# Three small operations of a fused state-space and attention kernel leave VectorE

## The chip, the cores and the metric

The kernel runs on one core of a Trainium2 chip. That core has five engines with a queue of instructions each, which they work off in order: TensorE (PE; its weight loads are a row of their own, PEld), VectorE (DVE), ScalarE (ACT), GpSimd (POOL) and SyncE (SP), which here only issues DMAs. An instruction that needs another engine's result waits for a semaphore, and everything behind it on its own engine waits with it. The metric is the device time of one execution in microseconds, the median of several runs; lower is better.

## The reference

The input x has 32 sequences of 256 tokens and 256 features. Two blocks follow each other, and their result is added to x.

The first is a selective scan. For every sequence, x is projected to 512 inner features and a gate; the inner features get a conditioning vector, a causal convolution of four taps, a SiLU and a layernorm over the 512 features. From the normalised `xn` come 16 values each of B, C and dt per token. The recurrence is

```python
dt = jnp.tanh(dt @ W_dt.T + b_dt) * 0.01
A = -jnp.tanh(A_log)
Ad = 1.0 + dt * A
h = jnp.clip(h * ad[:, :, None] + bd[:, :, None] * xt[:, None, :], -10.0, 10.0)
yt = jnp.einsum('bd,bdh->bh', ct, h)
```

with 256 steps, one per token. Its output, with a skip term, is gated and projected back to 256 features.

The second block is two layers, each of local attention (8 heads of 64, windows of 128 tokens that also see the window before) and a gated feed-forward (682 hidden features, GELU). Queries and keys are normalised per head, `t / clip(norm(t), 1e-12)`, scaled and rotated before the scores.

## The kernel before

**Groups and stages.** The 32 sequences are worked in four groups of eight. The scan of a group holds its state as 128 rows (16 states times 8 sequences) by 512 features. `group_scan` cuts its 256 steps into eight chunks of 32. While attention and feed-forward of one group run, the scan of the next one runs beside them. So the first group's scan runs alone at the start, the last group's attention alone at the end, and between them both share the engines. A pair of sequences in attention goes with one chunk of the scan.

**What sets the order.** `at(slot, function, ...)` puts a function of the scan into a numbered slot, counted in steps; `stage(n, i, ...)` does the same for attention and feed-forward; the loop at the end interleaves the two lists. That gives the program order. The framework then moves instructions of an engine against each other where their dependences allow, except those marked `tc.keep_in_program_order`. Tiles come from rings of a few buffers, and all eight PSUM banks are one ring (`ps_w`): a matmul that takes a bank waits until whoever read that bank's last content is done.

**The scan's layernorm, per chunk and half `j`.** The convolved features are turned by TensorE into PSUM (`tp_x`, L548). `norm_stats` (L555 on) takes mean and variance on VectorE (L558, L560), adds the epsilon (L562), and GpSimd raises it to the power -0.5 (L565); the result is the first column of `stat`. `norm_shift` (L571) makes minus mean times that factor on VectorE, the second column. `norm_apply` (L579) uses both as scale and bias of one ScalarE pass, which writes `xn`. GpSimd then applies the layernorm's weights (`norm_affine`, L586 and L587), and the rows go to DRAM (`xnd`), from where every step's row is read again, spread over the states (`xrep`, L685).

**The decay factors, per chunk.** From small sums (`bcd`) ScalarE takes the tanh (`decay_th`, L643); `decays` multiplies by a rate per row and adds one (L648), takes the running product `pd` (L650), its reciprocal (L653) and from it the factor `beta` (L654), with which ScalarE scales every `xrep` (L706). A step of the scan is then one VectorE instruction, an addition with limits (L716), and TensorE reads the state out (`y`, L728). The limits `lim` are the clip divided by the product (L660, L661, on GpSimd).

**Queries and keys.** `rotated` (L998 on) is called for q and k of each window of 128 tokens. ScalarE squares the projection (L1002); VectorE makes the two rotated parts (L1005, L1010) and sums the squares per head into `ss` (L1015), 128 rows by 8 heads, limited from below at 1e-24 (L1019). GpSimd adds the parts (L1013), raises `ss` to -0.5 (`rn`, L1021) and multiplies (L1022). TensorE transposes the result (L1028).

**Others that the text speaks of.** L1386 is the gelu on ScalarE, L1393 the product with the other half on VectorE (it frees the bank `pa`), L1047 the addition to the residual, L1252 and L1260 the softmax's sums and their reciprocal `rinv`, L1271 the weighted values `ov`, L799 the scan's gate `zT`, L758 its skip product.

Of the kernel before, what the change touches and what calls it, by code (L numbers as in the profile page):

```python
# [10 lines left out]
FP = mybir.dt.float32  # L11
BF = mybir.dt.bfloat16
I32 = mybir.dt.int32
AF = mybir.ActivationFunctionType
ALU = mybir.AluOpType
# [4 lines left out]
P = 128  # L20
# [53 lines left out]
def kernel(  # L74
# [29 lines left out]
    nc = tc.nc  # L104
# [38 lines left out]
    a_sb = per_state(a_log, "a_sb")  # L143
# [24 lines left out]
    one = const.tile([P, 1], FP, tag="one", name="one")  # L168
# [53 lines left out]
    def program(ctx, exact):  # L222
# [3 lines left out]
        sm = ctx.enter_context(tc.tile_pool(name="sm", bufs=2, reuse_waits="tile"))  # L226
# [150 lines left out]
        def group_scan(g):  # L377
# [14 lines left out]
            def at(s, what, *args):  # L392
                agendas[-1].setdefault(s, []).append(partial(what, *args))
# [161 lines left out]
            def norm_stats(c, j):  # L555
                tp, stat = ck[c]["tp", j], ck[c]["stat"]
                st = sm.tile([P, 6], FP, tag="st", name="st")
                nc.vector.bn_stats(st, tp)  # L558
                mv = sm.tile([P, 2], FP, tag="mv", name="mv")
                nc.vector.bn_aggr(mv, st)  # L560
                ve = sm.tile([P, 1], FP, tag="ve", name="ve")
                nc.vector.tensor_scalar_add(  # L562
                    ve, mv[:, 1:2], LN_EPS if alone else 4 * LN_EPS
                )
                nc.gpsimd.tensor_tensor(stat[:, j, 0:1], ve, neg_half[:, 0:1], ALU.pow)  # L565
                ck[c]["mv", j] = mv

            def norm_shift(c, j):
                stat, mv = ck[c]["stat"], ck[c].pop(("mv", j))
                tc.keep_in_program_order(  # L570
                    nc.vector.scalar_tensor_tensor(  # L571
                        stat[:, j, 1:2], mv[:, 0:1], -1.0, stat[:, j, 0:1], ALU.mult, ALU.mult
                    )
                )

            def norm_apply(c, j):
# [64 lines left out]
            def decay_th(c):  # L641
                ad = sm.tile([P, CH], FP, tag="ad", name="ad")
                nc.scalar.activation(ad, ck[c]["bcd"][:, 2], AF.Tanh, bias=wbias[:, 2:3])  # L643
                ck[c]["ad"] = ad

            def decays(c):
                ad, bcd, beta = ck[c].pop("ad"), ck[c].pop("bcd"), ck[c]["beta"]
                nc.vector.tensor_scalar(ad, ad, a_sb, 1.0, ALU.mult, ALU.add)  # L648
                pd = sm.tile([P, CH], FP, tag="pd", name="pd")
                nc.vector.tensor_tensor_scan(pd, ad, zero_ch, state["p"], ALU.mult, ALU.add)  # L650
                state["p"] = pd[:, CH - 1 : CH]
                pi = sm.tile([P, CH], FP, tag="pi", name="pi")
                nc.vector.reciprocal(pi, pd)  # L653
                nc.vector.tensor_mul(beta, beta, pi)  # L654
                ct = sm.tile([P, CH], FP, tag="ct", name="ct")
                nc.vector.scalar_tensor_tensor(
                    ct, bcd[:, 1], wbias[:, 1:2], pd, ALU.add, ALU.mult
                )
                lim = sm.tile([P, 2, CH], FP, tag="lim", name="lim")
                nc.gpsimd.tensor_scalar_mul(lim[:, 0], pi, CLIP)  # L660
                nc.gpsimd.tensor_scalar_mul(lim[:, 1], pi, -CLIP)  # L661
                ck[c].update(ct=ct, lim=lim)
# [193 lines left out]
            for c in range(NCH):  # L856
                s0 = c * CH
                for hb in range(CH // TB):
                    s = s0 + hb * TB
                    for i in range(NI):  # L860
                        at(s + 4 * i + 5, read_out, c, hb, i)
                    at(s + 21, gated, c, hb)
                    at(s + 25, out_gate, c, hb)
                    at(s + 11, skip, c, hb)
                for ch in range(NC_):
                    at(s0 - 38 + 2 * ch, conv_in, c, ch)
                    at(s0 - 37 + 2 * ch, conv_taps, c, ch)
                    at(s0 - 36 + 2 * ch, conv_th, c, ch)
                    if not alone:
                        at(s0 - 35 + 2 * ch, conv_out, c, ch)  # L870
                for ch, s in enumerate((13, 16, 17, 18)):
                    at(s0 + s + 2, gate_th, c, ch)
                    if not alone:
                        at(s0 + s + 4, gate_out, c, ch)
                at(s0 - 25, raw_copy, c)
                at(s0 - 24, raw_turn, c)
                for j in range(NJ):
                    s = s0 - 26 + 4 * j
                    at(s + 2, norm_stats, c, j)
                    at(s + 4, norm_shift, c, j)  # L880
                    at(s + 5, norm_apply, c, j)
                    at(s + 6, norm_affine, c, j)
                    at(s + 9, norm_out, c, j)
                at(s0 - 11, length, c)
                at(s0 - 9, figures, c)
                at(s0 - 7, figures_in, c)
                at(s0 - 6, decay_th, c)
                at(s0 - 5, decays, c)
                at(s0 - 4, put_c, c, 0)
                at(s0 + 4, put_c, c, 1)  # L890
                for d in range(KM):
                    at(s0 + 45 + 2 * d, copy_y, c, d)
                    at(s0 + 46 + 2 * d, put_y, c, d)
# [104 lines left out]
        def rotated(l, ps, w, a):  # L998


            sq = ap_.tile([P, DI], FP, tag="swp", name="sq", bufs=3)
            nc.scalar.activation(sq, ps, AF.Square)  # L1002
            rot = ap_.tile([P, HEADS, DH], FP, tag="rot", name="rot", bufs=4)
            ph = ps.rearrange("p (h d) -> p h d", h=HEADS)
            nc.vector.tensor_mul(rot, ph, bc(rc_sb[:, l, w, a], 1, HEADS))  # L1005
            swp = ap_.tile([P, HEADS, DH], FP, tag="swp", name="swp", bufs=3)
            hd = DH // 2
            for i in range(2):
                o, s = slice(i * hd, (i + 1) * hd), slice((1 - i) * hd, (2 - i) * hd)
                nc.vector.tensor_mul(  # L1010
                    swp[:, :, o], ph[:, :, s], bc(rs_sb[:, l, w, a, o], 1, HEADS)
                )
            nc.gpsimd.tensor_add(rot, rot, swp)  # L1013
            ss = aw.tile([P, HEADS], FP, tag="ss", name="ss")
            nc.vector.tensor_reduce(  # L1015
                ss, sq.rearrange("p (h d) -> p h d", h=HEADS), AX.X, ALU.add
            )

            nc.vector.tensor_scalar_max(ss, ss, 1e-24)  # L1019
            rn = aw.tile([P, HEADS], FP, tag="rn", name="rn")  # L1020
            nc.gpsimd.tensor_tensor(rn, ss, neg_half, ALU.pow)  # L1021
            nc.gpsimd.tensor_mul(rot, rot, bc(rn, 2, DH))  # L1022
            return rot
# [638 lines left out]
```

## Time and profile before

| | us |
|---|---|
| median of 3 runs (lowest, highest) | 3594.73 (3590.82, 3597.36) |
| profiled execution, its own time | 3592.27 |
| its span | 3590.5 |
| TensorE busy | 3448.4 |
| VectorE busy | 2667.8 |
| ScalarE busy | 1979.5 |
| GpSimd busy | 1874.5 |

The span begins with the first instruction on the core and ends with the last. In the groups of instructions a row is one line of the kernel, its engine and operation, the tiles written and read, and the count; then the time busy in total, the mean of one in ns, the engine's idle time just before them and what ended most of it. Matmuls are pipelined, so the mean of one matmul is longer than its share. In a view of waits, "PE ov L1271 <- DVE ag L1393" is TensorE idle ahead of line 1271 until VectorE had finished line 1393, with the sum, the number of times and the longest. The chain that ended last follows the work back from the last instruction, at each step to what released it. TensorE's granted clock was 0.99 of full speed.

### The profile page before, as it was taken

The page shows a single profiled execution, that of the slowest core. Times are in us where ns is not written, and L with a number is a line of the kernel's source. Part 1 is how long each engine was busy: PE and PEld are TensorE (multiplying, and loading weights), DVE is VectorE, ACT ScalarE, POOL GpSimd, SP SyncE. Part 2 cuts the span into 40 slices and gives each one's busy share as a digit, 9 for nine tenths or more (in the row PEclk, how much of TensorE's full clock was granted, in tenths as well). Part 3 has the DMA queues.
Part 4 walks back from the last instruction along what each step waited for, and adds up shares of the span by engine and source line. Part 5 has one row for each costly group of instructions (what it writes and reads, how often), then busy time and mean ns, then how long its engine had stood idle before and what let it go on. Part 6 is the DMA issues. An engine that isn't in the chain of part 4 may idle for free.

```text
span 3590.5 us, 57544 instructions
## 1 busy us (share of the span) xinstructions
PE 3448.4 (96%) x20220; PEld 2253.8 (63%) x20220; DVE 2667.8 (74%) x5049; ACT 1979.5 (55%) x3535; POOL 1874.5 (52%) x1842
## 2 busy tenths in 40 slices
PE   7999989999999999999999999999999999999999
PEld 4545335566656666666666666666666677777777
DVE  5888989878788877877787888777777555555553
ACT  4656656656555655566566555665656444434442
POOL 4433467546556556655555566555545454544551
PEclk9999999999999999999999999999999999999999
DMA  7788755444444555444454555534353112011111
GB/s 201 215 209 220 201 156 151 131 112 139 129 134 127 147 146 142 138 117 125 118 140 127 135 149 139 146 107 130 113 143 118 56 49 64 13 30 36 34 27 37
DMA packets 468766, 435.67 MB, mean 121 GB/s; under 512 B 228723, under 2 KB 308084, under 8 KB 468340
## 3 DMA queue, kind: packets, MB, share of 16 engines
q1 hardware_dynamic: 384018, 419.88, 41.9%
q10 hardware_dynamic: 84450, 12.01, 2.0%
q8 instruction: 163, 2.67, 0.3%
q14 instruction: 135, 1.11, 0.1%
HBM read 383.54 MB, written 46.66 MB: 120 GB/s over the span
## 4 chain that ended last, share of the span: by engine, by line
PE 62%; DVE 19%; DMA 7%; POOL 5%; issue 3%; ACT 3%; SPq 1%; ACTq 0%; DVEq 0%; POOLq 0%
PE pa L1375 13%; PE ps_qkv L989 13%; DVE h L716 7%; PE po_f L1402 7%; PE ps_wo L1039 5%; DMA xrep<-xnd 5%; PE y L728 4%; PE ov L1271 3%; PE sc L1215 3%; PE ps_out L808 2%; PE ps_in L399 2%; PE tr_qk L1028 2%; PE rs L1252 2%; DVE acc L489 2%; PE ps_raw L518 1%
## 5 line engine op out<-in xcount | busy, mean ns | idle before, releaser
L716 DVE CUSTOM_DVE_ANT_0 h<-h,xrep,lim 128x512 f32<-128x512 f32 x1024 | 956.3, 934 | 195.5 <-ACT xrep L706 164.6
L706 ACT ACTIVATE xrep<-xrep,beta 128x512 f32<-128x512 f32 x960 | 673.6, 719 | 358.8 <-DMA xrep<-xnd 258.4
L989 PE MATMUL ps_qkv<-qkv,res 128*128 128x512 f32 x1536 | 713.5, 600 | 18.9 <-DVE rinv L1260 8.2
L1375 PE MATMUL pa<-hT,w 128*128 128x256 f32 (+1 forms) x2816 | 675.1, 382 | 11.8 <-DVE zT L799 11.4
L1375 PEld LDWEIGHTS pa<-hT,w 128*128 128x128 f32 (+1 forms) x2816 | 516.8, 188 | 153.6 <-issue 35.0
L1013 POOL TENSOR_TENSOR rot<-rot,swp 128x512 f32<-128x512 f32 x256 | 341.5, 1334 | 448.9 <-DVE swp L1010 399.5
L1021 POOL TENSOR_TENSOR rn<-ss,neg_half 128x8 f32<-128x8 f32 x256 | 466.3, 1822 | 16.7 <-DVE ss L1019 7.0
L989 PEld LDWEIGHTS ps_qkv<-qkv,res 128*128 128x128 f32 x1536 | 281.8, 191 | 302.3 <-issue 239.6
L728 PE MATMUL y<-h,ly 128*32 128x512 f32 x2048 | 347.2, 611 | 14.9 <-DVE h L716 13.9
L1327 POOL TENSOR_TENSOR rstd<-ve,neg_half 128x2 f32<-128x2 f32 x64 | 46.6, 727 | 524.6 <-DVE ve L1325 508.4
L1402 PE MATMUL po_f<-ag,w 128*128 128x256 f32 x1280 | 307.4, 387 | 6.9 <-DVE fo L1413 4.0
L1022 POOL TENSOR_TENSOR rot<-rot,rn 128x512 f32<-128x512 f32 x256 | 287.4, 1123 | 19.9
L1393 DVE SCALAR_TENSOR_TENSOR ag<-pa,b_sb,ag 128x256 f32<-128x256 f32 x320 | 151.6, 474 | 181.2 <-ACT ag L1386 181.0
L1402 PEld LDWEIGHTS po_f<-ag,w 128*128 128x128 f32 x1280 | 235.9, 191 | 72.0 <-issue 12.0
L1386 ACT ACTIVATE ag<-pa,b_sb 128x256 f32<-128x256 f32 x320 | 150.4, 470 | 232.6 <-PE pa L1375 231.5
L1002 ACT ACTIVATE sq<-ps_qkv 128x512 f32<-128x512 f32 x256 | 151.5, 596 | 199.8 <-PE ps_qkv L989 132.4
L489 DVE SCALAR_TENSOR_TENSOR acc<-xr,wc_sb,acc 128x256 f32<-128x256 f32 x384 | 196.9, 536 | 51.0 <-POOL acc L478 50.5
L1005 DVE TENSOR_TENSOR rot<-ps_qkv,rc_sb 128x512 f32<-128x512 f32 x256 | 174.9, 683 | 78.1 <-ACT sq L1002 77.7
L1039 PE MATMUL ps_wo<-oT,wo 128*128 128x256 f32 x1024 | 231.6, 379 | 0.0
L1039 PEld LDWEIGHTS ps_wo<-oT,wo 128*128 128x128 f32 x1024 | 194.5, 190 | 27.2 <-ACT sq L1002 0.8
L1227 ACT ACTIVATE pT<-sc 128x512 f32<-128x512 f32 x384 | 202.4, 603 | 7.8 <-PE sc L1215 6.0
L1271 PE MATMUL ov<-pT,v_sb 128*64 128x256 f32 (+1 forms) x2048 | 184.3, 330 | 19.3 <-DVE ag L1393 19.3
(159 smaller groups left out, 5462.8 us busy)
## 6 DMA issues: line engine op xcount, KB each, us to landing
xrep<-xnd SPq DMA_DIRECT2D x960, 256.0 KB
rb<-inv SPq DMA_DIRECT2D x128, 256.0 KB
xnd<-xn SPq DMA_DIRECT2D x64, 256.0 KB
qkv<-in_wqkv_dram SPq DMA_DIRECT2D x24, 512.0 KB
ahead<-xs_a SPq DMA_DIRECT2D x48, 256.0 KB
xp<-ahead SPq DMA_DIRECT2D x48, 256.0 KB
xd<-xnd SPq DMA_DIRECT2D x192, 64.0 KB
w<-in_w_dram SPq DMA_DIRECT2D x80, 128.0 KB
```

The costliest lines, as they stand in the source:

```text
L489: nc.vector.scalar_tensor_tensor(acc, xr[:, :, k : k + CH], wc_sb[:, ch, k : k + 1], acc, ALU.mult, ALU.add,)
L706: scaled = nc.scalar.activation(bx, ck[c].pop(("bx", t), bx), AF.Copy, scale=ck[c]["beta"][:, t : t + 1])
L716: nc.vector._custom_dve(TENSOR_ADD_SAT, out=h_new, in0=state["h"], in1=bx, s0=ck[c]["lim"][:, 0, t : t + 1], s1=ck[c]["lim"][:, 1, t : t + 1],
L728: nc.tensor.matmul(ck[c]["y", hb][32 * q : 32 * q + 32, :], ly[hb % 2][:, 32 * t : 32 * t + 32], ck[c].pop(("h", hb * TB + t)), start=(i = ...
L989: nc.tensor.matmul(ps, res[b][:, k, t0 : t0 + W], wt["qkv", a][:, k], start=(k == 0), stop=(k == KM - 1),)
L1013: nc.gpsimd.tensor_add(rot, rot, swp)
L1021: nc.gpsimd.tensor_tensor(rn, ss, neg_half, ALU.pow)
L1022: nc.gpsimd.tensor_mul(rot, rot, bc(rn, 2, DH))
L1039: nc.tensor.matmul(po[:, d], wt["wo", 0][:, c, d * P : (d + 1) * P], oT[:, c, :], start=(c == 0), stop=(c == NC_ - 1),)
L1271: nc.tensor.matmul(ov[r * DH : (r + 1) * DH, i, kw * W :], self.qkv[b][2][:, kw, h * DH : (h + 1) * DH], self.p.pop((b, kw, i0 + i, r)), s ...
L1375: nc.tensor.matmul(dst[x], wt["w1", m][:, k, x], self.h[:, k], start=(k == 0), stop=(k == KM - 1),)
L1402: nc.tensor.matmul(self.po[:, d], wt["w2", 0][:, m, d * P : (d + 1) * P], self.ag[m], start=(m == 0), stop=(m == len(MCH) - 1),)
```

## The change

It has three parts.

- The lower limit of `ss` (L1019) is computed by GpSimd with the same operation.
- The tanh of the decay factors is completed by ScalarE: an Identity activation with the rate as scale and a column of ones as bias, in place. The VectorE instruction in `decays` goes.
- `norm_stats` makes minus the mean on VectorE in a tile `nm` of its own, and `norm_shift` multiplies it by the factor from GpSimd in a ScalarE Copy activation. It isn't held to program order any longer, and its slot moves from s + 4 to s + 5, that of `norm_apply`.

```diff
                 nc.gpsimd.tensor_tensor(stat[:, j, 0:1], ve, neg_half[:, 0:1], ALU.pow)
-                ck[c]["mv", j] = mv
+                nm = sm.tile([P, 1], FP, tag="nm", name="nm")
+                nc.vector.tensor_scalar_mul(nm, mv[:, 0:1], -1.0)
+                ck[c]["nm", j] = nm
 
             def norm_shift(c, j):
-                stat, mv = ck[c]["stat"], ck[c].pop(("mv", j))
-                tc.keep_in_program_order(
-                    nc.vector.scalar_tensor_tensor(
-                        stat[:, j, 1:2], mv[:, 0:1], -1.0, stat[:, j, 0:1], ALU.mult, ALU.mult
-                    )
+                stat = ck[c]["stat"]
+                nc.scalar.activation(
+                    stat[:, j, 1:2], ck[c].pop(("nm", j)), AF.Copy, scale=stat[:, j, 0:1]
                 )
...
                 nc.scalar.activation(ad, ck[c]["bcd"][:, 2], AF.Tanh, bias=wbias[:, 2:3])
+                nc.scalar.activation(ad, ad, AF.Identity, bias=one, scale=a_sb)
                 ck[c]["ad"] = ad
 
             def decays(c):
                 ad, bcd, beta = ck[c].pop("ad"), ck[c].pop("bcd"), ck[c]["beta"]
-                nc.vector.tensor_scalar(ad, ad, a_sb, 1.0, ALU.mult, ALU.add)
...
                     at(s + 2, norm_stats, c, j)
-                    at(s + 4, norm_shift, c, j)
+                    at(s + 5, norm_shift, c, j)
                     at(s + 5, norm_apply, c, j)
...
-            nc.vector.tensor_scalar_max(ss, ss, 1e-24)
+            nc.gpsimd.tensor_scalar_max(ss, ss, 1e-24)
             rn = aw.tile([P, HEADS], FP, tag="rn", name="rn")
             nc.gpsimd.tensor_tensor(rn, ss, neg_half, ALU.pow)
```

## The prediction

> **What bounds the kernel now.** I read the busy shares first, then busy time by stage, then TensorE's waits in the steady stage, then the groups of the edited lines and the timeline of one stall. Shares of the whole span:
>
> ```profile
> PE 3448.4 (96%) x20220; PEld 2253.8 (63%) x20220; DVE 2667.8 (74%) x5049; ACT 1979.5 (55%) x3535; POOL 1874.5 (52%) x1842
> ```
>
> By stage (columns: window and its length, then busy time of PE, PEld, DVE, ACT, POOL; clock, DMA share, GB/s):
>
> ```profile
> 75.00:440.00 365.00, 340.16 (x1444) 171.84 (x1444) 314.68 (x558) 230.65 (x416) 141.24 (x190) 0.96 0.79 212
> 440.00:700.00 260.00, 233.67 (x1277) 125.88 (x1278) 231.31 (x422) 154.52 (x282) 158.86 (x163) 0.97 0.54 150
> 700.00:1600.00 900.00, 863.02 (x5325) 566.96 (x5324) 729.63 (x1370) 531.70 (x959) 507.93 (x490) 1.00 0.48 132
> 1600.00:2700.00 1100.00, 1073.25 (x6651) 713.03 (x6650) 871.33 (x1672) 656.59 (x1184) 627.85 (x585) 1.00 0.48 131
> ```
>
> From 2700 us on PE shows 100% in every slice of 100 us up to 3500: no gain is there. The rest has four kinds of time: the first scan alone (A, to 440), a transition whose busiest engines are DVE and PE, 89% and 90% (B, 440 to 700), and scan beside attention (C, 700 to 1600; D, 1600 to 2700). TensorE is idle 260.0 - 233.7 = 26.3 us in B, 37.0 in C, 26.8 in D; these 90 us are about all that the change can win there. In D a pair of sequences, one scan chunk of 32 steps, takes 101.4 to 103.7 us with 99.5 to 99.9 of PE work. What ends TensorE's waits in D (us in total, times, longest):
>
> ```profile
> PE ov L1271 <- DVE ag L1393: 12.3, 9, 1.4
> PE ps_qkv L989 <- DVE rinv L1260: 5.8, 9, 0.9
> PE pa L1375 <- DVE zT L799: 4.6, 4, 1.2
> PE ps_qkv L989 <- DVE xd L779: 2.6, 9, 0.6
> ```
>
> VectorE, 79% busy, ends all of them: its queue is late, not full. The instructions that leave it (busy us, mean ns | idle before):
>
> ```profile
> L1019 DVE TENSOR_SCALAR ss<-ss 128x8 f32<-128x8 f32 x256 | 118.2, 462 | 0.6
> ...
> L648 DVE TENSOR_SCALAR ad<-ad,a_sb 128x32 f32<-128x32 f32 x32 | 22.0, 689 | 10.9 <-ACT ad L643 10.9
> ...
> L571 DVE SCALAR_TENSOR_TENSOR stat<-mv,stat 128x1 f32<-128x1 f32 x64 | 18.6, 290 | 60.6 <-POOL stat L565 60.6
> ```
>
> And the largest stall, in order of time:
>
> ```profile
> 1677.67 1.02 DVE L1019 TENSOR_SCALAR ss<-ss 128x8 f32<-128x8 f32 x1
> ...
> 1682.12 1.02 DVE L648 TENSOR_SCALAR ad<-ad,a_sb 128x32 f32<-128x32 f32 x1
> ...
> 1685.00 0.45 DVE L1393 SCALAR_TENSOR_TENSOR ag<-pa,b_sb,ag 128x256 f32<-128x256 f32 x1
> ...
> 1685.60 1.52 PE L1271 MATMUL ov<-pT,v_sb 128*64 128x256 f32 x16 [1.38 <-DVE ag L1393]
> ```
>
> The last gelu ahead of it on ScalarE was done at 1676.6; L1393 was late only because of what stood ahead of it on VectorE, two of the moved instructions among them.
>
> **What the Trainium skill says.** "SBUF — State Buffer", Who interferes with whom: a tensor_scalar on VectorE can take the port pair that it shares with GpSimd, and one fully blocks the other; two SBUF inputs also contend with GpSimd's reads. The trace agrees: L648 takes 232 to 1021 ns and L1019 151 to 1076, so the small operations are waits for GpSimd more than work, and L571 once takes 1229 instead of 156. "ScalarE: Activation LUTs", Table sets: copy and identity are in every set, so no table load is added; the issue order of the changed kernel has the 126 loads of the trace.
>
> **The change, part by part.**
>
> *Limit on GpSimd.* VectorE loses 256 x 462 ns = 118.2 us: 13.4 in B, 37.5 in C, 44.5 in D, 22.9 after 2700, where cover is complete. GpSimd gains 256 small tensor_scalars. No such row exists at 128x8: 128x32 takes 314 ns (L660) or, right behind it, 485 (L661, median 620), and a memset of 128x8 takes 105. So 0.11 to 0.62 us; I take 0.35, near L660 with some blocking: +90 us on POOL, from 52% to about 55%. In its queue stand rn (L1021) and rot (L1022), then often the pow of the scan's layernorm (L565), on which ScalarE waits. Where GpSimd waits for VectorE a rotation's chain changes by 0.35 - 0.46 = -0.1 us; where it has a backlog, by +0.35. After 2700 the first rotation of a pair ends at 2961.9 and its transposes start at 2969.1: 7 us of cover against 0.7.
>
> *Decay factors on ScalarE.* VectorE loses 32 x 689 = 22.0 us. ScalarE gains 32 ACTIVATEs with two pointers on 32 columns; "ScalarE: Activation LUTs", What ACT_TABLE_LOAD costs, gives 186 + 2 x 93 + 27 = 399 ns (estimate); its 306 for one pointer stands against 319 measured at L643. So +13 us on ACT, and the scan L650 waits for it directly. Behind it on ACT stand xrep scalings; on DVE the beta that those need. In A, where L648 costs only 241 ns and DVE already waits 10.9 us for L643 (6 times), each of 8 chunks loses about 0.4 - 0.24 = 0.15: +1 us. In C and D it saves its 1.0 us.
>
> *Shift on ScalarE.* VectorE loses 64 x 290 = 18.6 us and gains 64 negations at the 144 ns of L562, 9.2 us. More: VectorE no longer stands 60.6 us waiting for L565. ScalarE gains 64 x 280 ns (186 + 93 + 1, same section) = 18 us. It waits at the shift where it waited at xn (L579: 144.2 us for L571), so that wait stays. The issue order puts the first xn of a chunk about three instructions earlier, ahead of a gelu and a square: GpSimd's two affine operations (2.6 us) then run in its 4.3 us of idle time instead of ahead of the rotation's add, but that gelu comes about 2.6 us later and the square 1.4 us, of which L1019's absence gives 0.9 back to the second swp: up to 0.5 us lost per pair on PSUM banks.
>
> No transfer is added or removed; SP issues the same 1917 rows, the order within a pair shifts by one to three places from 700 us on. In B conv taps move ahead by up to 44 places on DVE, past the first rotations: a loss of up to 4 us once, a gain of as much.
>
> *The sum.* In D, L1393 of the stall above stands behind 0.34 + 1.02 (two L1019) + 1.02 (L648) = 2.4 us less, but the new order puts L653, L656, L654 and L1047 ahead of it: 0.34 + 0.15 + 0.19 + 0.67 = 1.35. So it is 1.0 us earlier, or 2.0 if the L716 between them is no longer stretched (1.83 us against its usual 0.81); I let the 1.38 go. D: -12.3 (ov), -2.9 (half of rinv: its cause is partly the xrep transfers), +2.2 (11 pairs x 0.2, half the loss at the first xn): **-13**. C: DVE ends 28 of its 37 us; on the chain that ended last stand 7.9 of L1019, 1.5 of L648, 2.0 of L571 = 11.4, less 10 rn on the chain x 0.35 = 3.5, plus what an unblocked VectorE gives (it waited 20.0 us for L565 there; I take a sixth, 3): **-11**. B: 4.1 + 0.9 on the chain, less 6 rn x 0.35 = 2.1, plus a third of the other 9.3 us of L1019: **-6**. A: **+1**. Sum -29. Against the profiled execution (3592.3, span 3590.5 and 1.8 around it) 3563; it lies 2.5 under the median of the runs, so **3566**.
>
> **Rivals.**
>
> *More than that (0.08).* All waits of B to D that DVE ends go, and half of the others: about -65, 3530. For it: beta comes some 4 us earlier at 1686, ScalarE waits 34.6 us for it in D. Against: 0.5 us per pair of new lateness, and xrep transfers (66.8 us of ACT's waits in D) that nothing shortens.
>
> *No change (0.12).* PE is 96% busy; when L1393 is on time the next late thing takes its place: rinv, zT, or the square behind xn. 3590 to 3595. For it: several waits share one place. Against: the largest has its cause in the moved instructions.
>
> *Slower, by GpSimd's queue (0.12).* Between 1620 and 1630 us GpSimd runs two rotations and a skip product, then L565, and ScalarE stands 7.07 us at xn with gelus and xrep behind it. Two limits put this off by 2t, the ACTIVATE adds 0.1. With t = 0.62 that is 1.3 us in each of 24 chunks beside attention, +32 us if PE has no slack there, less 15 of the gain: 3612. It decides from t of about 0.6, or from 0.35 if the early xn costs its full 0.5 too. Against: PE shows no wait in that stretch now.
>
> *The change doesn't do what it says:* a negation stays on VectorE, 9.2 us, costed above; the rest leaves.
>
> **How the numbers follow.** The forecast, -8 to -50, has 0.68; its own range is 3545 to 3586. The cases above hold 0.32. A difference of 0.2%, 7.2 us, is what a measurement can tell from none. Faster: 0.68 + 0.08 + 0.01 of the no-change case = 0.77; slower 0.12 and 0.01 = 0.13; the same 0.10. The bounds of t alone (0.11 to 0.62) move 16 rn on the chain by -4 to +4 us. Range 3536 to 3598: below it half of the larger gain, above it most of the slower case.
>
> **What will show it.** TensorE's wait for ag L1393 at ov falls from 19.3 us to under 8; a pair in D takes 100.5 to 101.5 us; DVE busy falls by 150 us; its wait for L565 is gone; POOL's new group has a mean of 270 to 450 ns; the tail after the scan is as long as before. Wrong: the limit at 0.6 us or more, ScalarE's wait ahead of the shift above 170 us, or new PE waits for swp and ag just after the first xn of a chunk.

## The result, and the profile after it

The changed kernel takes 3601.67 us, the kernel before 3597.49 us beside it (medians of 20 runs each): a ratio of 1.0013, 95% interval 1.0005 to 1.0021. The forecast was 3566 us and a range up to 3598. So the change makes a difference too small to count, on the slow side: 29 us of gain were forecast and a loss of 4 us was measured, 33 us apart.

Busy shares of the changed kernel's profiled execution (span 3596.5 us, 3590.5 before), and the same four stages (columns as before: window and its length, busy time of PE, PEld, DVE, ACT, POOL, then clock, DMA share, GB/s):

```profile
PE 3459.6 (96%) x20220; PEld 2255.0 (63%) x20220; DVE 2571.2 (71%) x4761; ACT 2008.9 (56%) x3631; POOL 1960.4 (55%) x2098
```

```profile
75.00:440.00 365.00, 340.01 (x1441) 169.99 (x1442) 316.87 (x554) 236.67 (x436) 144.35 (x189) 0.98 0.79 210
440.00:700.00 260.00, 236.86 (x1306) 128.89 (x1308) 223.84 (x400) 158.01 (x292) 175.25 (x186) 0.94 0.54 149
700.00:1600.00 900.00, 867.49 (x5300) 570.23 (x5301) 691.74 (x1291) 538.93 (x983) 521.46 (x554) 0.99 0.48 132
1600.00:2700.00 1100.00, 1071.60 (x6614) 705.64 (x6613) 826.51 (x1558) 662.53 (x1209) 648.18 (x667) 1.00 0.48 130
```

VectorE has 96.6 us less to do, 44.8 of them in stage D, as the change meant. TensorE is none the less idle for 1100.0 - 1071.6 = 28.4 us of D, where it was idle for 26.8. (In B and C, by the same windows, its idle time fell from 26.3 to 23.1 us and from 37.0 to 32.5, at a lower granted clock than before: 0.94 for 0.97, and 0.99 for 1.00.) What ends its waits in D has changed:

```profile
PE ps_qkv L989 <- DVE rinv L1260: 7.5, 10, 0.9
PE ps_qkv L989 <- DVE ag L1393: 6.6, 8, 0.9
PE pa L1375 <- DVE zT L799: 4.0, 6, 1.2
PE ov L1271 <- ACT xn L579: 3.1, 10, 0.3
PE ps_qkv L989 <- DVE xd L779: 2.7, 10, 0.5
PE tr_qk L1028 <- DVE ag L1393: 2.0, 2, 1.5
```

The 12.3 us of ov waiting for ag are gone. In their place stand ps_qkv and tr_qk waiting for ag (8.6 us, 0.5 before), 1.7 us more for rinv and 3.1 us for xn. The edited lines, as groups (busy us, mean ns of one | idle time before it, and what ended it):

```profile
L1019 POOL TENSOR_SCALAR ss<-ss 128x8 f32<-128x8 f32 x256 | 101.5, 397 | 0.1
...
L572 ACT ACTIVATE stat<-nm,stat 128x1 f32<-128x1 f32 x64 | 18.7, 293 | 177.5 <-POOL stat L565 175.3 <-DMA rw<-raw 2.1
...
L644 ACT ACTIVATE ad<-ad,one,a_sb 128x32 f32<-128x32 f32 x32 | 13.2, 411 | 0.9
...
L567 DVE TENSOR_SCALAR nm<-mv 128x1 f32<-128x1 f32 x64 | 8.9, 140 | 0.0
```

Each is close to its forecast price (350 ns, 280, 399, 144). And at the place of the largest stall before, ov now runs straight through, with L1393 still behind the four instructions that the forecast named:

```profile
1682.06 2.90 PE L1271 MATMUL ov<-pT,v_sb 128*64 128x256 f32 x32
1682.22 0.34 DVE L653 RECIPROCAL pi<-pd 128x32 f32<-128x32 f32 x1
1682.48 0.15 DVE L656 SCALAR_TENSOR_TENSOR ct<-bcd,wbias,pd 128x32 f32<-128x32 f32 x1
1682.60 0.19 DVE L654 TENSOR_TENSOR beta<-beta,pi 128x32 f32<-128x32 f32 x1
1682.71 0.68 DVE L1047 TENSOR_TENSOR res<-res,ps_wo 128x512 f32<-128x512 f32 x1
1683.31 0.48 DVE L1393 SCALAR_TENSOR_TENSOR ag<-pa,b_sb,ag 128x256 f32<-128x256 f32 x1
```

So the steps worked and the time did not come. To see where it went, I measure in the traces from one start of ps_wo (L1039, the output projection of a sequence) to the next. There are 64 of these starts, one for each of the 32 sequences in each of the two layers; "sequence 19" in what follows is the 19th of them. A pair of sequences has two such halves: the one in which the scan's layernorm runs (the norm half) and the one in which the next chunk's decay factors are made (the decay half). From sequence 19 to 42, which is stage D and a little before it, a norm half took 51.78 us before and takes 52.26, a decay half 50.47 and 50.67 (means of 11; the stretch holds a twelfth norm half). From the first ps_qkv to the first ps_wo it went from 90.9 to 88.1 us, from there to sequence 19 from 955.1 to 959.6, through D from 1176.5 to 1184.4, and from there to the last ps_wo from 855.3 to 855.3. (In C the granted clock was 1.00 before and 0.99 after, so that these 4.5 us may be the clock, all the more as TensorE's idle time in C fell; in D it was 1.00 in both.) The stretches are steadier than the total: the first ps_qkv starts anywhere from 471 to 492 us among the kernels profiled here, which share stage A but for small edits, and the total inherits that. The stretch from the first ps_wo to sequence 19 is not much steadier: it takes 952 to 965 us in the first nine kernels of the table below.

### The profile page after: what moved, and what is told of

The parts are those of the page before. It is cut to its first block, busy times and chain, and to the rows that moved or that the text cites. A ratio compares the mean times of both kernels' runs of the same rounds, so it can differ in the third digit from the quotient of the medians.

```text
span 3596.5 us, 57665 instructions
## 1 busy us (share of the span) xinstructions
PE 3459.6 (96%) x20220; PEld 2255.0 (63%) x20220; DVE 2571.2 (71%) x4761; ACT 2008.9 (56%) x3631; POOL 1960.4 (55%) x2098
## 4 chain that ended last, share of the span: by engine, by line
PE 53%; DVE 16%; POOL 12%; DMA 9%; ACT 5%; issue 3%; SPq 0%; ACTq 0%; POOLq 0%; DVEq 0%
PE ps_qkv L989 12%; PE pa L1375 11%; DMA xrep<-xnd 7%; DVE h L716 7%; PE po_f L1402 6%; PE ov L1271 4%; PE y L728 3%; PE ps_wo L1039 3%; POOL rot L1013 3%; POOL rn L1021 3%; PE sc L1215 2%; ACT xrep L706 2%; DVE acc L489 2%; PE ps_in L399 2%; PE ps_out L808 2%
## 5 line engine op out<-in xcount | busy, mean ns | idle before, releaser
L716 DVE CUSTOM_DVE_ANT_0 h<-h,xrep,lim 128x512 f32<-128x512 f32 x1024 | 953.4, 931 | 293.6 <-ACT xrep L706 261.1
L1013 POOL TENSOR_TENSOR rot<-rot,swp 128x512 f32<-128x512 f32 x256 | 365.5, 1428 | 472.9 <-DVE swp L1010 424.3
L1021 POOL TENSOR_TENSOR rn<-ss,neg_half 128x8 f32<-128x8 f32 x256 | 441.3, 1724 | 21.3
L1393 DVE SCALAR_TENSOR_TENSOR ag<-pa,b_sb,ag 128x256 f32<-128x256 f32 x320 | 152.0, 475 | 213.1 <-ACT ag L1386 213.0
L1022 POOL TENSOR_TENSOR rot<-rot,rn 128x512 f32<-128x512 f32 x256 | 274.7, 1073 | 20.1
L1002 ACT ACTIVATE sq<-ps_qkv 128x512 f32<-128x512 f32 x256 | 150.8, 595 | 183.4 <-PE ps_qkv L989 118.4
L1039 PE MATMUL ps_wo<-oT,wo 128*128 128x256 f32 x1024 | 232.2, 380 | 1.2 <-DVE ag L1393 1.0
L1010 DVE TENSOR_TENSOR swp<-ps_qkv,rs_sb 128x256 f32<-128x256 f32 x512 | 191.7, 416 | 33.3 <-POOL rot L1013 32.9
L1039 PEld LDWEIGHTS ps_wo<-oT,wo 128*128 128x128 f32 x1024 | 194.0, 190 | 30.5 <-DVE ag L1393 3.6
```

The costliest lines, as they stand in the source:

```text
L716: nc.vector._custom_dve(TENSOR_ADD_SAT, out=h_new, in0=state["h"], in1=bx, s0=ck[c]["lim"][:, 0, t : t + 1], s1=ck[c]["lim"][:, 1, t : t + 1],
L1039: nc.tensor.matmul(po[:, d], wt["wo", 0][:, c, d * P : (d + 1) * P], oT[:, c, :], start=(c == 0), stop=(c == NC_ - 1),)
```

## The experiments

They are shown with their results in one table, and then in the order in which they were made. "M" stands for the limit on GpSimd, "F" for the decay factors on ScalarE (D in the labels), "S" for the shift on ScalarE; MFS is the changed kernel. "Bias" does the limit inside the square (below), "chain" forces ScalarE's scalings of the scan's rows into step order (last part). Stretch D is from sequence 19 to 42; it and both halves are in us. The granted clock there was 1.00 in every profile but those of T4 and BT4, where it was 0.99 (see there).

| kernel | label | ratio to before | 95% interval | stretch D | norm half | decay half |
|---|---|---|---|---|---|---|
| before | | 1 | | 1176.5 | 51.78 | 50.47 |
| MFS, the change | | 1.0013 | 1.0005 to 1.0021 | 1184.4 | 52.26 | 50.67 |
| M | e1_M | 0.9985 | 0.9978 to 0.9993 | 1179.1 | 52.49 | 49.94 |
| F | e1_D | 0.9991 | 0.9980 to 1.0002 | 1174.9 | 51.78 | 50.32 |
| S | e1_S | 0.9993 | 0.9984 to 1.0001 | 1177.5 | 51.81 | 50.53 |
| FS | e1_DS | 1.0002 | 0.9993 to 1.0011 | 1176.9 | 51.89 | 50.36 |
| MS | e1_MS | 0.9975 | 0.9965 to 0.9984 | 1175.5 | 52.28 | 49.84 |
| MF | e1_MD | 1.0031 | 1.0018 to 1.0044 | 1184.2 | 52.48 | 50.43 |
| FS, no limit | e2_NDS | 0.9948 | 0.9935 to 0.9961 | 1170.4 | 51.78 | 49.91 |
| bias, F, S | e4_BDS | 0.9948 | 0.9934 to 0.9961 | 1170.2 | 51.78 | 49.89 |
| MFS, row CH - 4 late | e5_T4 | 1.0043 | 1.0029 to 1.0058 | 1196.7 | 51.92 | 52.17 |
| MS, row CH - 3 early | e5_R33 | 0.9983 | 0.9973 to 0.9993 | 1182.7 | 52.32 | 50.49 |
| bias, F, S, row CH - 4 late | e5_BT4 | 0.9976 | 0.9965 to 0.9987 | 1181.4 | 51.78 | 50.91 |
| bias, S | e5_BS | 0.9902 | 0.9888 to 0.9917 | 1158.8 | 51.79 | 48.85 |
| MFS, chain | e7_C | 0.9864 | 0.9843 to 0.9884 | 1151.8 | 51.91 | 48.09 |
| MS, chain | e7_MSC | 0.9862 | 0.9841 to 0.9883 | 1150.5 | 51.92 | 47.97 |
| bias, F, S, chain | e7_BDSC | 0.9809 | 0.9792 to 0.9826 | 1144.6 | 51.78 | 47.57 |
| bias, S, chain | e7_BSC | 0.9818 | 0.9799 to 0.9836 | 1143.5 | 51.78 | 47.46 |
| before, chain | e7_0C | 0.9895 | 0.9875 to 0.9916 | 1161.8 | 51.78 | 49.13 |
| FS, chain | e7_DSC | 0.9916 | 0.9896 to 0.9936 | 1165.1 | 51.82 | 49.39 |

### One part alone, and the limit taken away

My theory after reading the trace was that the limits lengthen GpSimd's queue: L565, the power on which the scan's layernorm waits, ended 8.51 us after the start of ps_wo at 1622, and 7.52 before. The rival was the shift on ScalarE, which brings xn ahead of a gelu. The third was that each removed wait is only followed by another. The edits are the change's own, one at a time:

```diff
 # e1_M
-            nc.vector.tensor_scalar_max(ss, ss, 1e-24)
+            nc.gpsimd.tensor_scalar_max(ss, ss, 1e-24)
 # e1_D
                 nc.scalar.activation(ad, ck[c]["bcd"][:, 2], AF.Tanh, bias=wbias[:, 2:3])
+                nc.scalar.activation(ad, ad, AF.Identity, bias=one, scale=a_sb)
 ...
-                nc.vector.tensor_scalar(ad, ad, a_sb, 1.0, ALU.mult, ALU.add)
 # e1_S: nm on VectorE, norm_shift on ScalarE and its slot s + 5, as in the change
 # e2_NDS: the change without
-            nc.gpsimd.tensor_scalar_max(ss, ss, 1e-24)
```

> Only the limit on the squared lengths moves to GpSimd; decay factors and layernorm shift stay on VectorE. Queue theory (GpSimd's two limits of each chunk put the pow L565 about 1 us off, and with it xn, xrep and the gelus): this part alone is slower than the kernel before, by 3 to 12 us, and ScalarE's wait ahead of xn for the chain of L565 grows from 78.6 to above 95 us in the stretch 1600 to 2700. Early-xn theory (the shift on ScalarE moves xn ahead of a gelu and that costs the gain): this part alone is faster, by 3 to 10 us, since VectorE loses its 118 us of L1019. Next-wait theory (every wait removed is followed by another one just behind it): within 3 us of before.

> Only the decay factors are completed on ScalarE. Queue theory and early-xn theory alike: faster by 2 to 8 us, because 22 us leave VectorE ahead of L1393 at the largest stall and nothing is added to GpSimd's queue. Next-wait theory: within 2 us, the wait of ov for ag falls by some 4 us or more in 1600 to 2700 and the waits of ps_qkv for ag and rinv grow by as much.

> Only the layernorm's shift goes to ScalarE. Queue theory: within 3 us of before, since GpSimd has no new work. Early-xn theory: slower by 3 to 10 us, with the gelu that follows the first xn of a chunk about 2 us later and PE waits for ag behind it. Next-wait theory: within 3 us.

> The change with the limit on squared lengths (1e-24) left out altogether: neither VectorE nor GpSimd computes it, decay factors and shift are on ScalarE as in the changed kernel. Queue theory: what the limit costs on GpSimd is gone, so the time is 15 to 35 us below that of the changed kernel, 3565 to 3588. Early-xn theory: the loss stays, 3592 or more. Next-wait theory: 3588 to 3602, that is within 7 us of before.

None of the parts costs anything alone: 0.9985, 0.9991 and 0.9993 (M's interval alone leaves out 1), together 0.31% below before, where all three at once are 0.13% above. So the queue theory, which had M slower by itself, and the early-xn theory, which had S slower, both fail as explanations of the whole. M's trace also missed the sign that it named: ScalarE's wait ahead of xn grew from 78.6 to 92.2 us, not to above 95. Half of the queue theory is true, though. The norm half is 52.26 to 52.49 us in M, MS, MF and MFS and 51.78 to 51.89 in the kernels without the limit on GpSimd, so the limits do cost about 0.5 us there in each pair. And leaving the limit out of the change brings 3586.16 us, within the queue theory's range. What makes the parts worse together than alone is not in it.

The next-wait theory describes F's trace. The stall of ov for ag went, as expected there, but the waits of ps_qkv for rinv shrank (from 5.8 to 4.5 us) instead of growing, and ov itself found another wait in D:

```profile
PE ov L1271 <- DVE res L1047: 14.7, 9, 1.6
```

It replaces the 12.3 us for ag; FS has the same wait. So the decay factors alone, though they leave VectorE, make stretch D only 1.6 us shorter (1176.5 to 1174.9).

### Two parts at a time, and the limit for nothing

```diff
 # e1_DS, e1_MS, e1_MD: the kernel before with two of the three edits above
 # e4_BDS: the change, with
+    tiny = const.tile([P, 1], FP, tag="tiny", name="tiny")
+    nc.gpsimd.memset(tiny, 1e-12)
 ...
-            nc.scalar.activation(sq, ps, AF.Square)
+            nc.scalar.activation(sq, ps, AF.Square, bias=tiny)
 ...
-            nc.gpsimd.tensor_scalar_max(ss, ss, 1e-24)
```

> The changed kernel with the limit back on VectorE; TensorE's order of instructions is that of the changed kernel. Each part alone measured at or a little below the time of before (0.9985, 0.9991, 0.9993), so the loss comes from parts together. Queue theory (limit on GpSimd delays L565, and ScalarE then stands at the shift): the limit is the part that costs, this kernel is at 0.994 to 0.999 of before, and from the first wo of sequence 19 to that of 42 takes 1170 to 1177 us against 1184.4. ScalarE theory (decay factors and shift, together 32 us more on ScalarE, delay gelus and xrep): 1.000 to 1.003, and that stretch takes 1180 us or more.

> Limit on GpSimd and shift on ScalarE, decay factors back on VectorE. Queue theory: the limit and the shift together make the loss, 1.000 to 1.003 of before. ScalarE theory: without the decay factors the loss is gone, 0.997 to 0.999.

> Limit on GpSimd and decay factors on ScalarE, shift back on VectorE at its old place. Queue theory with ScalarE standing at xn as in before: the limit's delay is there but not the early xn, 0.998 to 1.001. Early-xn theory: this is the version without the loss, 0.995 to 0.998. ScalarE theory: 0.997 to 0.999.

> The changed kernel with the instruction of the limit dropped and its task done by a bias of 1e-12 inside the square that ScalarE computes already (a sum of squares can then not be zero): no instruction on VectorE or GpSimd, one pointer more on 256 squares of ScalarE. Queue theory: as with the limit left out (0.9948), 0.994 to 0.997. If the pointer costs ScalarE about 0.1 us on each square (estimate from ACTIVATEs with one and two pointers, 293 and 411 ns), 26 us more on ScalarE, ScalarE theory: 0.998 to 1.001.

The loss comes with F, but only where VectorE no longer has the limit. Adding F to M takes it from 0.9985 to 1.0031, to MS from 0.9975 to 1.0013: 0.4 to 0.5% (14 to 17 us). Adding F to the kernel before or to S changes it by -0.1 to +0.1%. In stretch D this is all in the decay half: 49.84 us for MS, 50.67 for MFS, but 50.53 for S and 50.36 for FS. (One of MFS's 11 decay halves holds a halved clock; without that pair the difference is 0.7 us instead of 0.8.) No theory had this. The ratios of FS and MS lie where the ScalarE theory put them, but FS's stretch of 1176.9 us doesn't (1180 or more), and MF at 1.0031 is outside every expectation.

The bias costs ScalarE 91 ns on each square (mean 686 ns in BS against 595 in the changed kernel, a price near the 93 ns per pointer of the Trainium skill, "ScalarE: Activation LUTs", What ACT_TABLE_LOAD costs), and is as good as leaving the limit out: 0.9948. Queue theory had that right.

### What F changes on ScalarE

The same decay half of MS and of MFS, ScalarE in order of time, first MS (ps_wo starts at 1883.69):

```profile
1889.48 0.32 ACT L643 ACTIVATE ad<-bcd,wbias 128x32 f32<-128x32 f32 x1 [2.36 <-DVE bcd L632]
1889.70 0.71 ACT L706 ACTIVATE xrep<-xrep,beta 128x512 f32<-128x512 f32 x1
1890.32 0.56 ACT L1033 COPY qT<-tr_qk 128x512 f32<-128x512 f32 x1
1890.78 0.58 ACT L1033 COPY kT<-tr_qk 128x512 f32<-128x512 f32 x1
1891.26 0.73 ACT L706 ACTIVATE xrep<-xrep,beta 128x512 f32<-128x512 f32 x1
1894.91 0.72 ACT L706 ACTIVATE xrep<-xrep,beta 128x512 f32<-128x512 f32 x1 [2.92 <-DMA xrep<-xnd]
```

and MFS (ps_wo starts at 1880.59):

```profile
1886.40 0.32 ACT L643 ACTIVATE ad<-bcd,wbias 128x32 f32<-128x32 f32 x1 [2.84 <-DVE bcd L632]
1886.75 0.41 ACT L644 ACTIVATE ad<-ad,one,a_sb 128x32 f32<-128x32 f32 x1
1887.07 0.71 ACT L706 ACTIVATE xrep<-xrep,beta 128x512 f32<-128x512 f32 x1
1891.36 0.72 ACT L706 ACTIVATE xrep<-xrep,beta 128x512 f32<-128x512 f32 x1 [3.58 <-DMA xrep<-xnd]
1891.99 0.57 ACT L1033 COPY qT<-tr_qk 128x512 f32<-128x512 f32 x1
1892.45 0.59 ACT L1033 COPY kT<-tr_qk 128x512 f32<-128x512 f32 x1
1892.93 1.34 ACT L706 ACTIVATE xrep<-xrep,beta 128x512 f32<-128x512 f32 x2
...
1899.02 0.72 ACT L706 ACTIVATE xrep<-xrep,beta 128x512 f32<-128x512 f32 x1 [3.90 <-DMA xrep<-xnd]
```

The trace leaves out which row an xrep holds. The built programs' issue lists tell it (numbers: the step of the chunk whose row is scaled; a prime: of the next chunk; g: a gelu; ad: decay factors). All kernels of one line have the same list in steady chunks (NFS: FS with no limit):

```
before, F, S, FS, MS, BS 25 26 g 27 g ad     28     qT kT 29 0' 2' g    oT 4' oT 31    g qT kT v 1'
MF, MFS, NFS, BFS        25 26 g 27 g ad ad  28  0' qT kT 29    2' g    oT 4' oT 31    g qT kT v 1'
T4, BT4 (below)          25 26 g 27 g ad ad      0' qT kT 28 29    g 2' oT    oT 31 4' g qT kT v 1'
R33 (below)              25 26 g 27 g ad     28  29 qT kT 0' 2'    g 4' oT    oT 31    g qT kT v 1'
MFS, chain               25 26 g 27 g ad ad  28     qT kT 29 30    g    oT    oT 31 0' g qT kT v 1' 2'
```

(F and FS have two ad; row 30 is scaled earlier in all but the last.) So F with the limit off VectorE moves 0', the first row of the *next* chunk, ahead of the copies of qT and kT and of row 29, which VectorE needs next. The transfer of 0' is not there yet; ScalarE stands for 3.58 us with row 29 landed behind it. From here the delay can be followed, in us after the start of ps_wo, MFS against MS: row 29 is scaled at 12.34 instead of 7.57; VectorE's steps 29 and 30 start at 13.11 instead of 10.40:

```profile
1893.70 1.66 DVE L716 CUSTOM_DVE_ANT_0 h<-h,xrep,lim 128x512 f32<-128x512 f32 x2 [3.29 <-ACT xrep L706]
1895.28 0.48 DVE L1393 SCALAR_TENSOR_TENSOR ag<-pa,b_sb,ag 128x256 f32<-128x256 f32 x1
1895.67 1.75 DVE L1260 RECIPROCAL rinv<-rs 128x256 f32<-128x256 f32 x1
1900.87 0.81 DVE L716 CUSTOM_DVE_ANT_0 h<-h,xrep,lim 128x512 f32<-128x512 f32 x1 [3.45 <-ACT xrep L706]
```

Behind them the ag of 1895.28 and rinv are late (rinv at 15.08 instead of 14.06). The steps give the xrep buffers back late, so SyncE issues the next two transfers at 13.95 and 14.79 instead of 12.19 and 13.04; row 4' is scaled at 18.43 instead of 16.71, and the gelu two places behind it at 20.15 instead of 18.43. TensorE pays at three places: tr_qk waits 0.51 us for ag, ps_qkv 0.94 for rinv (0.73 in MS), the third ps_qkv 0.86 for ag (0.37). This half takes 51.16 us in MFS and 49.43 in MS. In stage D VectorE waits for xrep 148.2 us in MFS and 118.4 in MS, ScalarE for xrep's transfers 90.0 and 77.0.

### Shifting one scaling by a slot

Two edits were to test this: undo the exchange in MFS, and make it in MS, by moving one row's scaling by one slot. They were planned before the rows had been told apart, and moved other rows than the one that counts.

```diff
 # e5_T4 on the change, e5_BT4 on e4_BDS
-                    at(s0 + t - 2, scale_row, c, t)
+                    at(s0 + t - (1 if t == CH - 4 and not alone else 2), scale_row, c, t)
 # e5_R33 on e1_MS
+                    at(s0 + t - (3 if t == CH - 3 and not alone else 2), scale_row, c, t)
 # e5_BS: e4_BDS with the decay factors on VectorE as in before
```

> The changed kernel, and in each chunk beside attention the scaling of one row, that of step CH - 4, is issued one slot later; nothing else is edited. That puts ScalarE's copies of qT and kT, just behind the decay factors, ahead of the second xrep scaling instead of behind it, as they stand in the kernel without the decay factors on ScalarE (0.9975). Order theory (the decay factors cost through this exchange: the copies, and the step behind them, stand behind an xrep whose transfer lands late): 0.996 to 0.999 of before, 8 us or more below the changed kernel, and the second half of a pair in 1600 to 2700 takes 49.3 to 50.3 us where the changed kernel has 50.2 to 51.9. ScalarE theory (the 411 ns of the added ACTIVATE themselves cost, with the scan waiting for it): 1.000 to 1.002.

> Limit on GpSimd and shift on ScalarE, decay factors on VectorE as in before (0.9975), and in each chunk beside attention the scaling of the row of step CH - 3 is issued one slot earlier: ScalarE's order behind the tanh of the decay factors then has the second xrep scaling ahead of the copies of qT and kT, as in the changed kernel. Order theory: the loss comes without the added ACTIVATE, 1.000 to 1.003. ScalarE theory: 0.996 to 0.999.

> The changed kernel with the limit done by the bias of the square (0.9948) and the row of step CH - 4 one slot later. Order theory: another 5 to 10 us, 0.992 to 0.9945. ScalarE theory: 0.994 to 0.996.

> Limit done by the bias of the square, shift on ScalarE, decay factors on VectorE as in before; the old order of qT and kT against xrep stands by itself. Order theory: 0.991 to 0.9945, below the version with the decay factors on ScalarE (0.9948). ScalarE theory: the same range. If VectorE's load were what counts, the 22 us of the decay factors that stay on VectorE put it above that version, 0.995 to 0.997.

T4 and BT4 came out 0.3% *above* the kernels that they edit, R33 0.08% above, which its interval doesn't tell from nothing. The issue lists above say why. In T4 the row in front of the copies is still 0', and now 28 stands behind it too: ScalarE waits 3.20 us for 0' right behind the decay factors, and later 3.58 us for another with both copies of oT behind it, the second xrep wait here:

```profile
1903.63 0.72 ACT L706 ACTIVATE xrep<-xrep,beta 128x512 f32<-128x512 f32 x1 [3.20 <-DMA xrep<-xnd]
...
1910.49 0.72 ACT L706 ACTIVATE xrep<-xrep,beta 128x512 f32<-128x512 f32 x1 [3.58 <-DMA xrep<-xnd]
1911.12 1.05 ACT L1278 COPY oT<-ov 128x512 f32<-128x512 f32 x2
```

TensorE's waits in D are then ps_qkv for oT, 30.6 us of them, and a lower clock comes on top. In stage D (1600 to 2700) of these two traces TensorE stood 17 times for 2.1 us or longer, always for oT, and behind 15 of the 17 the granted clock was halved for 3.4 us or more. A matmul of ps_qkv then took up to 1223 ns instead of 592, and four of them took

```profile
1911.73 3.49 PE L989 MATMUL ps_qkv<-qkv,res 128*128 128x512 f32 x4 [2.73 <-ACT oT L1278]
```

where MFS needs 1.98 us for them behind a wait of 0.94. The other 18 traces have no wait of that length in stage D, and one halving in all. Of the 12.3 us by which stretch D is longer in T4 than in MFS, 5.0 are idle time of TensorE, and of BT4's 11.2 against BFS 6.1; the rest is longer matmuls. Over all its executions, too, T4 ran at a mean granted clock of 0.984 and BT4 at 0.986, all other kernels at 0.988 to 0.991.

In R33 the row in front of the copies is 29, which has landed and is due; only 4' in front of the first oT is new. (In its trace a decay half is 0.65 us longer than in MS; the time of 22 runs hardly shows that.) None of the four ratios lies where the order theory had put it, and R33's lies where the ScalarE theory had. Since other rows were moved than meant, these runs don't decide between an order and the 411 ns of the added ACTIVATE; they show that an xrep ahead of a copy costs when its transfer is late, the clock behind the wait included. BS, with the old list, is 35 us below before (0.9902), lower than either theory had it; BFS, which adds F and the new list, is 0.46% above BS.

### Scalings in step order

The clean test takes the rows' order away as a variable: each scaling beside attention is queued on ScalarE behind that of the step before.

```diff
-                scaled = nc.scalar.activation(
-                    bx, ck[c].pop(("bx", t), bx), AF.Copy, scale=ck[c]["beta"][:, t : t + 1]
-                )
+                with ExitStack() as behind:
+                    if "scaled" in state:
+                        behind.enter_context(tc.issue_after(state["scaled"]))
+                    scaled = nc.scalar.activation(
+                        bx, ck[c].pop(("bx", t), bx), AF.Copy, scale=ck[c]["beta"][:, t : t + 1]
+                    )
                 if not alone:
+                    state["scaled"] = scaled.ins
                     tc.keep_in_program_order(scaled)
```

The existing `keep_in_program_order` doesn't do this: it puts an instruction behind the one written just before it on that engine, and when that one is moved ahead, the pinned one can be too.

> The changed kernel with one edit: each xrep scaling beside attention is issued on ScalarE behind the scaling of the step before it (an order of issue, no wait for its end), so that no row of the next chunk is scaled ahead of an older row. Order theory (the decay factors cost because the next chunk's first row, whose transfer lands last, is put ahead of the copies of qT and kT and of an older row): 0.993 to 0.998 of before, at least 10 us below the changed kernel (1.0013), and VectorE's wait of h for xrep in 1600 to 2700 falls from 148 us to below 120. Time theory (the added 411 ns on ScalarE, with the scan waiting for it): 1.000 to 1.002. If scaling in step order itself delays what stood ahead: above 1.002.

> Limit on GpSimd and shift on ScalarE, decay factors on VectorE (0.9975 without the edit), with scalings in step order. Order theory: within 0.1% of the changed kernel with the same edit, both at 0.993 to 0.998. Time theory: 0.3 to 0.4% below it, as without the edit.

> Limit done by the bias of the square, decay factors and shift on ScalarE (0.9948 without the edit), scalings in step order. Order theory: 0.986 to 0.991, within 0.1% of the version without the decay factors on ScalarE. Time theory: 0.994 to 0.996, 0.4% above that version.

> Limit done by the bias of the square, shift on ScalarE, decay factors on VectorE (0.9902 without the edit), scalings in step order. Order theory: 0.986 to 0.991; some scalings stand out of step order here too, so that a gain of up to 0.4% is left in it. Time theory: 0.989 to 0.991.

With F and without it the kernels now come together, 0.9864 and 0.9862, and 0.9809 and 0.9818. So F's cost went with the order, as the order theory had it. The chain by itself would leave a way out, since TensorE hardly waits any more and might cover the ACTIVATE's 411 ns too. Against that stand F and FS, which have the ACTIVATE with the old order and no cost, and the delay followed above, which starts with the 3.58 us for 0'. The order is also worth far more than I had expected, more than any range above: the changed kernel falls from 1.0013 to 0.9864. The decay half of MFS is 48.09 us instead of 50.67, and the norm half 51.91 instead of 52.26. TensorE's waits in D with the chain (L992 is ps_qkv there, L1378 pa; three lines further down for the edit):

```profile
PE pa L1378 <- DVE zT L802: 4.7, 7, 1.6
PE ov L1274 <- DVE res L1050: 1.6, 1, 1.6
PE ps_wo L1042 <- DVE ag L1396: 0.8, 4, 0.2
PE ps_qkv L992 <- DVE rinv L1263: 0.7, 1, 0.7
```

8.2 us of idle time remain of 28.4, and of ScalarE's 90.0 us of waiting for xrep's transfers 2.5. One number was missed: VectorE still waits 128.4 us for xrep, not below 120. With TensorE idle for only 8.2 us, most of these waits are covered.

The last two runs ask what the change is worth once the order is settled:

```diff
 # e7_0C: the kernel before with the chain alone
 # e7_DSC: e1_DS with the chain
```

> The kernel before with scalings in step order and nothing else. If the order hid the whole worth of the change: 0.993 to 0.996 (the sum of 29 us forecast, 0.8%, then stands between this kernel and the changed one with the same edit, 0.9864). If the order is all there is and the three parts are worth nothing: 0.985 to 0.988.

> Decay factors and shift on ScalarE, limit on VectorE, scalings in step order. If the limit is better on GpSimd than on VectorE: above 0.988. If it costs GpSimd's queue as much as it frees on VectorE: 0.985 to 0.988. Below 0.985 if GpSimd's queue is what counts most.

The order alone brings the kernel before to 0.9895, between the two ranges: it scaled 30 before 25, and 0', 2' and 4' before 31, all along. Between this and MFS with the chain lie 0.31% in the times, 11 us, and the intervals overlap. In the two traces it is 24 us: 4.2 up to the first ps_wo (92.1 to 87.9), 10.1 from there to sequence 19 (943.6 to 933.5) and 10.0 in stretch D (1161.8 to 1151.8). Only the last is steady: from the first ps_wo to sequence 19 the four chained kernels with the limit off VectorE take anything from 933.0 to 941.0 us.

In D the gain is the limit's. TensorE's longest wait there is, in before with the chain and in FS with the chain,

```profile
PE ov L1274 <- DVE ag L1396: 12.4, 9, 1.4
PE ov L1274 <- DVE res L1050: 14.8, 9, 1.6
```

and with the limit off VectorE 1.6 us of it are left (MFS) or none (MS). So F and S together take 3.3 us more in stretch D (1161.8 to 1165.1), and M on top of them saves 13.3 (to 1151.8); in the times FS with the chain is 0.9916 and MFS 0.9864. Done in the square the limit is better still, 0.9809: the fastest kernel found, 3533.0 us against 3599.94.

## Why the prediction was wrong

*The prices of the moved instructions* held. The limit takes 397 ns on GpSimd (0.35 forecast, and POOL rose by 85.9 us where 90 were forecast), the ACTIVATEs 411 and 293 (399 and 280), the negation 140. VectorE's wait for L565 is gone with L571. DVE fell by 96.6 us and not by 150, though. About 25 us of the difference are instructions left on VectorE that got longer (L773 469 to 640 ns, L656 165 to 284), which the prediction allowed for only the other way, as L716 "no longer stretched". The rest is counting: neighbouring instructions overlap in the trace, busy time counts an overlap once, and the durations added up fell by 124.8 us.

*"So it is 1.0 us earlier, or 2.0 … I let the 1.38 go. D: -12.3 (ov)"*: the stall at ov did go, and L1393 stood behind the four instructions named. But without F, in MS, the decay half is only 0.63 us shorter than before, 7 us in D: the waits of ps_qkv and tr_qk for ag grow from 0.5 to 4.5 us. Only with the scalings in step order is the stall worth what was forecast (11.3 us in stretch D for MS, both chained).

*"Decay factors on ScalarE … In C and D it saves its 1.0 us"* is the step that failed, in two ways. First, that 1.0 us a chunk came to almost nothing. F alone puts ov's wait for res (14.7 us) in place of its wait for ag (12.3) and shortens stretch D by 1.6 us, and with the chain F makes a decay half 0.1 us longer (47.97 to 48.09, 47.46 to 47.57). Second, the sum left out what the part does to the order. The prediction priced the ACTIVATE and what it removes on VectorE, and named the xrep scalings behind it, but did not read the order of issue on ScalarE at that place. With the limit off VectorE as well, the order puts 0' ahead of the copies and row 29. That costs 50.67 - 49.84 = 0.83 us in each decay half, 9 us in D, against the -13 forecast for the whole stage.

*The sum* for D then reads: -7 for the decay half without F, +9 for the exchange, and +6 for the norm half (below), or 8 us more where 13 less were forecast; stretch D did become 7.9 us longer. Chained, where the exchange can't happen, the three parts bring 10.0 us in D, near the forecast, but by the limit and not by the decay factors. The 10.1 us up to sequence 19 (11 forecast for C) and the 4.2 before it (6 for B) come from single traces of stretches that scatter by almost as much, and the times show 11 us in all, not 29. So whether those two terms were right stays open.

*The limit at 0.35, "where it has a backlog, by +0.35"*: the sum had no term for the norm half, and left this to the rival *slower, by GpSimd's queue*. It came true there in part, from below its stated point of 0.6: the two limits ahead of L565 take 0.24 and 0.68 us, L565 ends 1.0 us later, ScalarE waits 177.5 us ahead of the shift (the sign of being wrong was 170), and a norm half is 0.48 us longer: 6 us in the 12 of stretch D. "PE shows no wait in that stretch now" was no cover: ov waits there for xn, 3.1 us in D. Part of it is order too, since the chain brings the half from 52.26 to 51.91, and T4's order to 51.92.

*"Up to 0.5 us lost per pair on PSUM banks" by the early xn*, taken at +2.2 us: not there. S alone has a norm half of 51.81 against 51.78, and TensorE shows no new waits for ag just after the first xn.

*A, +1*: can't be told, since the start of ps_qkv scatters by 21 us among the profiles. *The tail*: as forecast, 855.3 us in both. *A pair in D*, forecast at 100.5 to 101.5 us, takes 102.9.

*The rivals.* "No change" came nearest, though its 3590 to 3595 us was missed too. Its reason holds in part: the next late thing did take the place of the removed wait (res in F, ag at ps_qkv in M). The rest was an exchange that the change itself brought, and a queue. Why the order flips only with both parts was not tried; that the framework takes beta as ready sooner when VectorE has less to do is argued, not shown.

## What to carry to other kernels

Where a framework orders the instructions, an edit changes two things, the work and the order; compare the issue lists of *every* engine around the edit with the loop step that each entry belongs to, not only those of the engines that are priced. On an engine that works off its queue in order, look for an entry of a later step ahead of one that is due, above all if it waits for a transfer: such places cost 1% here before the change and 0.4% more after it. And when parts are each harmless and the whole is not, test them two at a time before explaining any one. Look at the granted clock of a stretch, too, before its length is put down to waits.

## What the runs showed of the hardware that was not expected

- Instructions on VectorE got longer when the limit left it. L773 (128x256) has a mean of 460 to 474 ns in the six kernels with the limit on VectorE and of 635 to 669 in the fourteen without it, whether GpSimd does the limit, the square, or nobody. Standing elsewhere against GpSimd's work is the likely reason; it wasn't tried by itself.
- The 128x8 limit on GpSimd is 248 ns at the median, but 397 in the mean and 1211 at most.
- A wait of TensorE could cost a second time. In stage D of all 20 traces the granted clock was halved for 3.4 us or more behind 15 of the 17 waits of 2.1 us or longer (all in T4 and BT4). Behind the 98 waits of 1.0 to 2.0 us there was one halving, in MFS, where one of 1.5 us and one of 0.9 stood close together. Before 1600 us the picture is less sharp, and no run tested by itself whether the wait brings the lower clock.
- A bias pointer on a 128x512 square costs ScalarE 91 ns, 23 us in all, and was cheaper for the whole kernel than 256 instructions of 0.4 us on an engine 55% busy: 0.9809 against 0.9864 with the chain.
